# One index conversion for each row scatter instead of one for two, and a wider spread of the scatters over the batch

## The chip, the core and the metric

The kernel runs on one core of a Trainium2 chip. The metric is device time in microseconds (us). The core has five engines that work side by side, each through its own list of instructions in the order in which the program was built: TensorE (PE, with its weight loads PEld), VectorE (DVE), ScalarE (ACT), GpSimd (POOL) and SyncE (SP). Transfers run on 16 DMA engines and are issued from the lists of SP, ACT and POOL.

## What is computed

x has 8 batches of 512 rows of 256 numbers, in fp32. Four layers are added to it one after the other, each on layer-normed x:

```
x = x + scan(norm(x))         # silu(x Win), h = 0.9 h + x Bp, y = h Cp + D x, y Wout
x = x + ffn(norm(x))          # mixture of 16 experts, 4 chosen for each row, plus 2 shared
x = x + attention(norm(x))    # causal, 16 heads of 16
x = x + ffn(norm(x))          # the same mixture again
```

In the mixture each row picks 4 of 16 experts by its router scores. Its output is the weighted sum of what the four experts give, plus what the shared experts give.

## The kernel before

There are four stages. `stretch(Scan())` runs the scan layer over the 8 batches, and beside it, one and two batches behind, all of the first mixture that needs no sorted rows: the norm, the router scores, the choices and the shared experts. `routed(0, ...)` then runs the chosen experts of the first mixture on sorted blocks of 128 rows. `stretch(Attention())` and `routed(1, ...)` do the same for the attention and the second mixture.

Between a stretch and its `routed` lie the sorted rows. For each batch b the rows, normed, with their weights and numbers behind them, stand in a tile called `sorted_m` (buffer tag "rows", two buffers, so that batch b+2 takes the buffer of batch b). They are written to a table `xg` in device memory, 128 rows at a time, by an indirect DMA that POOL issues with 128 row positions (L656). A batch takes 16 of them: 4 tiles of rows by 4 choices. This text calls them the train of a batch, and m_0 to m_7 are the trains of the batches 0 to 7 of a stretch. The positions are computed in fp32 by DVE (`choices_w`, L633) and have to be unsigned integers. For the batches 0 to 6 ACT converts them (L653, `slots`), two columns for two scatters at a time, since PACE is 2; the conversion is kept at its place in ACT's list, so that a scatter can't start before ACT has come to that place. For batch 7 DVE converts all 16 columns at once (L635).

The place of each piece of work in the lists is set by `beside`, which merges generators by the share of their work that is done, and by `timed`, which gives each step a place between 0 and 1 of the batch of the layer (L1212 to L1250). The train of batch b-2 is dealt out in the loop over b: its last steps of choosing at 0.1, 0.14 and 0.18, and its 16 scatters from 0.22 on, spread towards 0.86 (towards 0.66 in the last batch; L1226). Then a scheduler puts the instructions in the lists by its own estimate of when they become ready; only the conversions are held where they were recorded.

Other work on POOL in the scan stretch is: adding the output bias to the next batch's x (L448, four instructions), writing the row numbers into the next `sorted_m` (an iota, L520, which has to wait until the last scatter out of that buffer has landed), and the power -1/2 of the norms (L400, `rstd_m` for the route and `rstd_l` for the layer). DVE waits for `rstd_m` before it writes `sorted_m` (L403), and its list goes on with the scan: L471, L473 (`state_s`) and L477. ACT scales by the skip weight (L474, after `state_s`), copies the transposed `sorted_m` out of PSUM (`xT_m`, L368), and PE then forms the router scores from it (`pl_m`, L543). In the attention stretch POOL also fills the values' tile with ones (L976, `v_a`).

SP stores each finished batch of x (L1193) and the shared experts' sums (L939).

Of the kernel before, what the change touches and what calls it, by code (L numbers as in the profile page):

```python
# [17 lines left out]
NT = T // P  # L18
# [11 lines left out]
EG, TKG, TK = 4, 2, 4  # L30
# [23 lines left out]
CLIP = 10.0  # L54
KB, COLS = 9, 6
HALVED = 1597463007.0
PACE = 2
SENT = 4
HELD = 6
EARLY = 2  # L60
# [12 lines left out]
def tile_hybrid_block(  # L73
# [22 lines left out]
    nc = tc.nc  # L96
# [38 lines left out]
    def rows_of(part, b: int):  # L135
        return part[b * T : (b + 1) * T, :].rearrange("(t p) d -> p t d", p=P)
# [168 lines left out]
    def behind(*pieces):  # L305
        def steps():
            for piece in pieces:
                yield from piece.steps

        return Piece(sum(piece.columns for piece in pieces), steps())  # L310
# [17 lines left out]
    def timed(steps, *places):  # L328


        def scaled():
            now = 0
            for place in places:
                yield place - now
                now = place
                next(steps)
            for _ in steps:
                pass

        return Piece(1, scaled())  # L340

    def spread(first: float, last: float, many: int):
        return [first + (last - first) * k / many for k in range(many)]

    def some(steps, many: int):

        for _ in range(many):
            yield next(steps)

    def issue(piece):  # L350
        for _ in piece.steps:
            pass


    def turned(src, tag: str, into, copies, home=None):

        rows = src()
        if home is None:
            dst = work.tile([P, KD, T], FP, tag="kb4", name=f"xT_{tag}", bufs=KB)
        else:  # L360
            dst = home(f"xT_{tag}")
        into(dst)
        for k in range(KD):
            pt = bank([P, NT, P], f"pt_{tag}_{k}")
            for t in range(NT):
                nc.tensor.transpose(pt[:, t, :], rows[:, t, k * P : (k + 1) * P], ident)
            flat = pt.rearrange("p t q -> p (t q)")
            copies[k](dst[:, k, :], flat)  # L368
            yield T // 2
# [38 lines left out]
    def kb4(name: str):  # L408
        return work.tile([P, NT, D], FP, tag="kb4", name=name, bufs=KB)
# [145 lines left out]
    def choices(i: int, b: int, tag: str, held, paced: bool):  # L555
# [65 lines left out]
        def of_choices(values, tag: str):  # L621
            found = work.tile(shape, FP, tag="col", name=f"found_{tag}", bufs=COLS)
            nc.vector.tensor_mul(
                found,
                pick,
                values.unsqueeze(2).to_broadcast(shape),
            )
            got = small.tile([P, NT, TK], FP, tag="choices", name=f"choices_{tag}")
            nc.vector.tensor_reduce(got, found, AX.X, ALU.add)
            return got  # L630

        slots = small.tile([P, NT * TK], U32, tag="slots", name=f"slots_{tag}")
        places = of_choices(where, f"w{tag}").rearrange("p t k -> p (t k)")  # L633
# [13 lines left out]
        for t in range(NT):  # L647
            for k in range(TK):
                at = t * TK + k
                if paced and at % PACE == 0:  # L650

                    pair = slice(at, at + PACE)
                    tc.keep_in_program_order(nc.scalar.copy(slots[:, pair], places[:, pair]))  # L653
                free(
                    f"xg{i}",
                    nc.gpsimd.indirect_dma_start(  # L656
                        out=xg[i],
                        out_offset=bass.IndirectOffsetOnAxis(ap=slots[:, at : at + 1], axis=0),
                        in_=rows[:, t, :],
                        in_offset=None,  # L660
                    ),
                )
                yield

    def free(group: str, made):

        tc.declare_no_dep(made.ins, group=group, reason="rows of their own")
        tc.add_to_no_dep_group(group, made.ins)
# [503 lines left out]
    def stretch(layer):  # L1172


        i = layer.mixture
        xT, xn, made, routes, sends = {}, {}, {}, {}, []

        def norm(b: int):
            def place():
                xn[b] = kb4(f"xn_{i}_{b}")  # L1180
                return xn[b]

            return normed(b, f"l{i}_{b}", place)

        def turn(b: int):
            return turned(lambda: xn.pop(b), f"l{i}_{b}", lambda xnT: xT.update({b: xnT}), layer.copies)

        def project(b: int):
            made[b], piece = layer.project(b, xT.pop(b))
            return piece  # L1190

        def store(b: int):
            nc.sync.dma_start(out=rows_of(parts[i][0], b), in_=x_tiles[b])  # L1193

        def experts(b: int):
            return shared_experts(i, b, lambda: routes.pop(b).held["xnT"], i == 1)

        for b in range(layer.ahead):
            if b < layer.early:
                xT[b] = ready.pop(b)  # L1200
            else:
                layer.load(b)
                issue(Piece(0, norm(b)))
                issue(Piece(0, turn(b)))
            if b == 0:
                issue(project(b))
        def start_route(b: int):
            routes[b] = Route(i, b, layer.copies)
            store(b)
            return routes[b]  # L1210

        for b in range(B):  # L1212
            pieces = [layer.main(b, made.pop(b))]
            nxt, last = b + layer.ahead, b == B - 1
            fill = []
            if layer.ahead > 1 and not last:
                fill.append(project(b + 1))
            if b > 1:
                shared_sum = experts(b - 2)
                if last:  # L1220

                    each = shared_sum.columns // 12
                    rest = Piece((12 - HELD) * each, shared_sum.steps)
                    shared_sum = Piece(HELD * each, some(shared_sum.steps, HELD))
                fill.append(shared_sum)
                pieces.append(timed(sends.pop(), 0.1, 0.14, 0.18, *spread(0.22, 0.66 if last else 0.86, NT * TK)))  # L1226
            if fill:
                pieces.append(behind(*fill))
            if b > 0:
                r = start_route(b - 1)  # L1230
                pieces.append(timed(r.norm(), *spread(0.0, 0.12, NT), *spread(0.2, 0.28, NT)))
                sends.append(r.rest)
                if last:
                    pieces += [
                        timed(r.scores(), 0.35, 0.38, *spread(0.45, 0.5, NT)),
                        timed(some(r.rest, PICKS), *spread(0.52, 0.66, PICKS)),
                        timed(some(r.rest, 3 + SENT), 0.69, 0.71, 0.73, *spread(0.75, 1.0, SENT)),
                    ]
                else:
                    pieces += [  # L1240
                        timed(r.scores(), 0.42, 0.46, *spread(0.55, 0.6, NT)),
                        timed(some(r.rest, PICKS), *spread(0.66, 0.95, PICKS)),
                    ]
            if nxt < B:
                layer.load(nxt)
                pieces += [
                    timed(norm(nxt), *spread(0.32, 0.44, NT), *spread(0.56, 0.64, NT)),
                    timed(turn(nxt), 0.75, 0.79),
                ]
            issue(beside(*pieces))  # L1250
            if layer.ahead == 1 and nxt < B:
                issue(project(nxt))
        layer.end()

        r = start_route(B - 1)
        chain = 3 + PICKS
        issue(
            beside(  # L1260
                behind(rest, experts(B - 2)),
                timed(r.norm(by_vector=True), *spread(0.0, 0.05, 2 * NT)),
                timed(sends.pop(), *spread(0.0, 0.5, NT * TK - SENT)),
                timed(r.scores(), 0.2, 0.22, *spread(0.28, 0.33, NT)),
                timed(some(r.rest, chain + 8), *spread(0.36, 0.68, chain), *spread(0.7, 1.0, 8)),
            )
        )
        table = []
        issue(
            beside(  # L1270
                experts(B - 1),
                timed(r.rest, *spread(0.0, 0.5, NT * TK - 8)),
                timed(blocks(i, table), 0.03, 0.14, 0.26, 0.38),
            )
        )
        return table

    with banks_of(one=8):
        table = stretch(Scan())
        wqkv_sb, wo_sb = load_attention_weights()  # L1280
# [90 lines left out]
```

## Time and profile before

| what | value |
|---|---|
| median of 3 runs | 1802.87 us (1798.23 to 1807.11) |
| profiled execution | 1817.59 us, span in the trace 1815.9 us |
| busy: PE, PEld | 93%, 70% of the span |
| busy: DVE, ACT, POOL | 60%, 44%, 42% |
| scan stretch | about 0 to 390 us |
| first routed stage | about 390 to 800 us |
| attention stretch | about 800 to 1383 us |
| second routed stage | about 1383 to 1816 us |
| scatters of rows (L656) | 256 on POOL, 255.4 us busy, 998 ns each |
| conversions by ACT (L653) | 112 of two columns, 19.4 us busy, 191 ns each |

A line of the profile's timeline has the start in us, the duration, the engine, the line of the code, the operation, what it writes and reads, how many instructions were merged into the line, and in square brackets the engine's idle time just before, with what ended it. A line of the table of stretches has the stretch, its length, then busy time and number of instructions of PE, PEld, DVE, ACT and POOL, and then the granted TensorE clock (1.00 is full), the busy share of the DMA engines and what they moved in GB/s.

### The profile page before, as it was taken

Reading aid. Unit: us, or ns where it says so; the run is one execution under the profiler, and the core shown is the slowest. Engines: PE = TensorE matmul, PEld = TensorE weight load, DVE = VectorE, ACT = ScalarE, POOL = GpSimd, SP = SyncE. Lnnn points to the kernel's source line nnn. Section 1 sums busy time; section 2 is a strip of 40 time slices with the busy share of each in tenths; the row PEclk is TensorE's granted clock in tenths of the full one; section 3 lists DMA queues with packets and bytes.
Section 4 is the critical chain, followed back from the end, with each engine's and each line's share of the span. In section 5 each row is a group of like instructions: output and inputs, shape, how many; then the busy total and the mean of one; then the engine's idle time right before and its main releaser. Section 6 shows DMA issues by size and latency. Waiting matters only on the chain. (4 is left out here: it accounts for less than half of the span.)

```text
span 1815.9 us, 32773 instructions
## 1 busy us (share of the span) xinstructions
PE 1694.6 (93%) x10640; PEld 1264.8 (70%) x10640; DVE 1088.1 (60%) x3364; ACT 805.3 (44%) x1740; POOL 763.0 (42%) x665
## 2 busy tenths in 40 slices
PE   5899998889999999989999999999988999999991
PEld 3566665569999999954445545544456999999991
DVE  5877775535555655556776676666643555555552
ACT  2322222125555555545564454454413555555550
POOL 4255554525555655540031321322551555565542
PEclk9899998989999999989999999999998999999995
DMA  5443322525566665540011112122542655566557
GB/s 162 151 149 131 130 78 85 178 77 95 96 97 102 108 97 94 94 88 12 24 58 63 61 64 69 50 72 72 178 147 62 97 97 94 107 118 97 97 105 240
DMA packets 149997, 181.37 MB, mean 100 GB/s; under 512 B 16096, under 2 KB 136960, under 8 KB 149824
## 3 DMA queue, kind: packets, MB, share of 16 engines
q0 software_dynamic: 53136, 76.81, 23.3%
q1 hardware_dynamic: 94320, 96.12, 17.8%
q10 hardware_dynamic: 2368, 6.29, 0.9%
q8 instruction: 89, 1.46, 0.3%
q14 instruction: 84, 0.69, 0.1%
HBM read 81.62 MB, written 97.53 MB: 99 GB/s over the span
## 5 line engine op out<-in xcount | busy, mean ns | idle before, releaser
L850 POOL DMA_INDIRECT part<-rows x272 | 426.4, 1568 | 388.2 <-ACT rows L849 339.9
L656 POOL DMA_INDIRECT xg<-sorted_m,slots_m x256 | 255.4, 998 | 298.2 <-ACT slots_m L653 120.2
L813 PEld LDWEIGHTS ph<-rows,gate 128*128 128x128 f32 x2176 | 286.3, 193 | 16.0 <-ACT rows L803 1.4
L813 PE MATMUL ph<-rows,gate 128*128 128x128 f32 x2176 | 289.7, 276 | 0.6 <-ACT rows L803 0.6
L813 PE MATMUL ph<-rows,up 128*128 128x128 f32 x2176 | 288.5, 276 | 0.0
L841 PE MATMUL pyr<-w_all,rows 128*128 x1088 | 281.9, 381 | 5.4 <-DVE rows L823 3.3
L813 PEld LDWEIGHTS ph<-rows,up 128*128 128x128 f32 x2176 | 266.0, 193 | 0.0
L821 ACT ACTIVATE rows<-ph 128x256 f32<-128x256 f32 x272 | 104.5, 384 | 333.1 <-PE ph L813 330.2
L822 DVE TENSOR_TENSOR rows<-ph,rows 128x256 f32<-128x256 f32 x272 | 115.5, 424 | 202.6 <-ACT rows L821 168.9
L841 PEld LDWEIGHTS pyr<-w_all,rows 128*128 128x128 f32 x1088 | 185.6, 191 | 20.6 <-issue 5.2
L795 ACT COPY gate<-w_all 128x512 f32 x272 | 170.0, 627 | 13.5 <-SPq L883 2.6
L1047 ACT ACTIVATE w_all<-ps_a 128x1024 f32<-128x1024 f32 x128 | 124.4, 1021 | 82.0 <-PE ps_a L1036 69.9
L902 PE MATMUL pg_m<-xT_m,su_sb 128*128 128x512 f32 x256 | 134.4, 650 | 5.2 <-ACT expert_b L736 5.2
L849 ACT ACTIVATE rows<-pyr,gain 128x256 f32<-128x256 f32 x272 | 128.7, 473 | 20.7 <-PE pyr L841 16.9
L795 DVE COPY up<-w_all 128x512 f32 x272 | 118.5, 436 | 32.1 <-PE ph L813 16.2
L1036 PE MATMUL ps_a<-w_all 32*128 32x512 f32 (+3 forms) x1024 | 123.3, 476 | 6.8 <-ACT w_all L1047 5.4
L930 PE MATMUL pd_m<-sd_sb,act_m 128*128 128x256 f32 x512 | 121.8, 386 | 4.5 <-DVE act_m L921 4.5
L902 PE MATMUL pg_m<-xT_m,sg_sb 128*128 128x512 f32 x256 | 123.0, 603 | 0.0
L823 DVE TENSOR_TENSOR rows<-ph,rows 128x256 f32<-128x256 f32 x272 | 115.2, 424 | 8.5
L826 DVE SCALAR_TENSOR_TENSOR gain<-rows,expert_b 128x4 f32<-128x4 f32 x272 | 60.4, 222 | 98.9 <-ACT rows L849 84.9
L802 PE MATMUL pt<-ident,rows 128*128 128x128 f32 x544 | 104.9, 275 | 12.8 <-DMA rows<-xg 12.8
L930 PEld LDWEIGHTS pd_m<-sd_sb,act_m 128*128 128x128 f32 x512 | 96.8, 192 | 27.2 <-DVE act_m L921 5.7
(208 smaller groups left out, 2205.3 us busy)
## 6 DMA issues: line engine op xcount, KB each, us to landing
rows<-xg SPq DMA_DIRECT2D x272, 136.0 KB
part<-x SPq DMA_DIRECT2D x16, 512.0 KB
part<-ys_m SPq DMA_DIRECT2D x16, 512.0 KB
w_all<-in_L_ffn_gate_w_dram SPq DMA_DIRECT2D x24, 256.0 KB
w_all<-in_L_ffn_up_w_dram SPq DMA_DIRECT2D x24, 256.0 KB
w_all<-in_L_ffn_down_w_dram SPq DMA_DIRECT2D x24, 256.0 KB
xg<-zeros SPq DMA_DIRECT2D x34, 136.0 KB
part<-rows POOLq DMA_INDIRECT x272
```

The source lines that it names most:

```text
L656: nc.gpsimd.indirect_dma_start(out=xg[i], out_offset=bass.IndirectOffsetOnAxis(ap=slots[:, at : at + 1], axis=0), in_=rows[:, t, :], in_of ...
L795: copy(here, w_all[:, bass.ds(held[n][0] + half * KD * F, KD * F)])
L813: nc.tensor.matmul(ph[:, s, f * P : (f + 1) * P], lhsT=both[s][:, k * F + f * P : k * F + (f + 1) * P], rhs=rows[:, ROW + k * P : ROW + (k ...
L822: nc.vector.tensor_mul(act, ph[:, 0, :], act)
L823: nc.vector.tensor_mul(act, ph[:, 1, :], act)
L841: nc.tensor.matmul(py, lhsT=act[:, f * P : (f + 1) * P], rhs=w_all[:, bass.ds(w + 2 * KD * F + f * D, D)], start=(f == 0), stop=(f == KF - 1),
L849: nc.scalar.mul(rows[:, 0:D], py, gain[:, TK : TK + 1])
L850: nc.gpsimd.indirect_dma_start(out=parts[i][n % 2], out_offset=bass.IndirectOffsetOnAxis(ap=rows[:, D + 2 * TK : D + 2 * TK + 1].bitcast(U ...
L902: nc.tensor.matmul(dst, lhsT=w[:, k, f * P : (f + 1) * P], rhs=xnT[:, k, :], start=(k == 0), stop=(k == KD - 1),)
L930: nc.tensor.matmul(py[:, j, :], lhsT=acts[n][:, f, t * P : (t + 1) * P], rhs=shared[n][3][:, f, :], start=(n == 0 and f == 0), stop=(n == ...
L1036: nc.tensor.matmul(ps[j // 2][:, j % 2, col : col + n], lhsT=k_sb[w][r, o, c * P : (c + 1) * P], rhs=q_sb[r, o, c * P : T], start=True, st ...
L1047: nc.scalar.activation(es[two], ps[two][:, :, 0:cols], AF.Exp, scale=ATT_SCALE)
```

## The change

PACE becomes 1: each of the 16 scatters of a paced batch has a conversion of its own, of one column, just ahead of it. The spread of the scatters goes from 0.22 to 0.86 (0.66 in the last batch) over to 0.26 to 0.98 (0.74 in the last batch), so that two neighbours stand 0.045 of a batch apart instead of 0.04. A variable gets another name.

```
-PACE = 2
+PACE = 1
...
                 if paced and at % PACE == 0:
-                    pair = slice(at, at + PACE)
-                    tc.keep_in_program_order(nc.scalar.copy(slots[:, pair], places[:, pair]))
+                    some_at = slice(at, at + PACE)
+                    tc.keep_in_program_order(nc.scalar.copy(slots[:, some_at], places[:, some_at]))
...
-                pieces.append(timed(sends.pop(), 0.1, 0.14, 0.18, *spread(0.22, 0.66 if last else 0.86, NT * TK)))
+                pieces.append(timed(sends.pop(), 0.1, 0.14, 0.18, *spread(0.26, 0.74 if last else 0.98, NT * TK)))
```

`spread(first, last, 16)` gives the places first + (last - first) k / 16 for k from 0 to 15.

## The prediction

> **What bounds the kernel now.** I read the table of stretches first: it shows where PE isn't full. Its columns are described above.
>
> ```profile
> 80.00:296.00 216.00, 204.64 (x755) 132.17 (x753) 162.27 (x474) 61.70 (x143) 105.12 (x115) 0.96 0.36 125
> ...
> 900.00:1296.00 396.00, 392.28 (x2439) 198.43 (x2432) 262.35 (x816) 198.37 (x321) 110.43 (x114) 0.99 0.19 64
> ```
>
> The first is the part of the scan stretch with trains, the second that of the attention stretch. In attention PE is idle for 3.7 of 396 us: there is nothing to win there, and something to lose only if ACT comes late. In the scan PE is idle for 11.4 of 216 us and runs below its full clock. So the scan decides, and I went through its timelines, POOL first. This is one batch, train m_1 and what follows it:
>
> ```profile
> 129.51 1.04 POOL L656 DMA_INDIRECT xg<-sorted_m,slots_m  x1 [13.20 <-DVE act_m L921]
> 130.85 1.16 POOL L656 DMA_INDIRECT xg<-sorted_m,slots_m  x1 [0.30 <-issue]
> 132.35 1.27 POOL L656 DMA_INDIRECT xg<-sorted_m,slots_m  x1 [0.33 <-ACT slots_m L653]
> ...
> 151.83 0.96 POOL L656 DMA_INDIRECT xg<-sorted_m,slots_m  x1 [0.30 <-DMA xg<-sorted_m,slots_m]
> 154.50 0.16 POOL L520 IOTA sorted_m<- 128x32 int32 x1 [1.71 <-DMA xg<-sorted_m,slots_m]
> 155.97 1.04 POOL L400 TENSOR_TENSOR rstd_m<-rstd_m,neg_half 128x4 f32<-128x4 f32 x1 [1.32 <-DVE rstd_l L399]
> ...
> 197.77 0.16 POOL L520 IOTA sorted_m<- 128x32 int32 x1 [2.91 <-DMA xg<-sorted_m,slots_m]
> 197.91 1.04 POOL L400 TENSOR_TENSOR rstd_m<-rstd_m,neg_half 128x4 f32<-128x4 f32 x1
> ```
>
> The train is not paced by ACT: after its third scatter it runs back to back, 0.96 us and a gap of 0.30, so 1.27 us a slot. POOL then waits for the landing, does the iota, and only then `rstd_m`. The next batch (197.77) shows the same. DVE stands still for it, and what follows on ACT and PE closes a ring:
>
> ```profile
> 198.99 1.38 DVE L403 TENSOR_SCALAR sorted_m<-x,mv_m,rstd_m 128x256 f32<-128x256 f32 x4 [5.35 <-POOL rstd_m L400]
> ...
> 131.27 0.72 ACT L474 ACTIVATE xi_s<-xi_s,d_sb 128x512 f32<-128x512 f32 x1 [2.27 <-DVE state_s L473]
> 131.90 0.27 ACT L653 CAST slots_m<-choices_wm 128x2 uint32<-128x2 f32 x2
> 132.07 0.57 ACT L368 COPY xT_m<-pt_m 128x512 f32<-128x512 f32 x1
> ...
> 132.70 0.39 PE L543 MATMUL pl_m<-rw_sb,xT_m 128*128 128x16 f32 x2 [0.97 <-ACT xT_m L368]
> 134.87 3.76 PE L902 MATMUL pg_m<-xT_m,su_sb 128*128 128x512 f32 x4
> ```
>
> From the end of `rstd_m` (115.18) DVE works without a pause to the fourth `state_s`; ACT's L474 waits for that, the copy `xT_m` stands behind it, and PE's `pl_m` waits for the copy. The first scatter starts 14.33 us after `rstd_m` ends (129.51 less 115.18), and the train leads to the next `rstd_m`. The ends of `rstd_m` lie at 115.18, 157.01, 198.95, 239.48 and 281.88: 41.7 us a batch. PE without pauses needs 38.5 (its first `pz_s` of two batches at 154.70 and 193.19). **The ring through POOL bounds the scan, not PE.** Every second batch PE is ahead and waits at `pl_m`; the table of stretches, cut just after that wait and at the same place a batch later, shows what comes of it:
>
> ```profile
> 134.00:139.00 5.00, 5.00 (x14) 2.93 (x13) 1.60 (x5) 0.00 (x0) 3.78 (x5) 0.50 0.30 113
> ...
> 174.00:179.00 5.00, 5.00 (x26) 3.44 (x25) 3.85 (x9) 2.10 (x9) 3.90 (x4) 1.00 0.30 111
> ```
>
> PE got half its clock after a pause of 0.97 and one of 0.18 us, and its batch took 42.2 us (`pl_m` from 132.70 to 174.91) instead of 38.5. (The Trainium skill, "TensorE: Matmul & The Clock Gate", section "What's actually happening", lets the clock fall only after about 3.4 us of idle. By the rule the longer pauses below would cost themselves alone, and a slow batch its pause in place of about 3.5 us more; the trace disagrees, and my sum goes by the ring.)
>
> **The change, part by part.**
>
> *Conversions.* 14 paced trains get 16 in place of 8: 112 more. One takes 191 ns, but neighbours start 0.09 us apart (two merged last 0.27), so each adds 0.1 of ACT's time, 11 us in all, spread over an engine that is 29% busy in the scan part above and 50% in the attention part. Nothing waits for most of them. In the scan one more stands between L474 and the first copy `xT_m`: 0.1 us at each wait of `pl_m`, but not on the ring.
>
> *The head of the train, scan.* By the built order the first conversion moves from behind the third L474 to just ahead of it (about 2 us earlier), and the next three stand behind the fourth L474, where two stood. The first scatter gains nothing: it waits for DVE (13.20, `act_m`), not for its conversion. The second one loses: it used the first pair, and now needs the conversion at 131.90. It can start where the third starts now, at 132.35 instead of 130.85. From there the train is back to back as before, so everything in it is **one slot later: 1.27 us** (bounds: nothing if the first scatter waited as long, and 132.35 to 133.92, 1.57, if the slow slot at the head recurs; I take 1.27, the rate of the other slots).
>
> *The tail of the train, scan.* The twelfth conversion follows the copy `xT_l` at 147.56, so at about 148.1; its scatter would be due at 146.76 + 1.27 = 148.03 and with the 0.45 us from conversion to scatter (131.90 to 132.35) starts at 148.5: 0.4 us more in the batches where PE was slow (m_1, m_3); in the others (conversion at 186.6, scatter due at 190.1) nothing. The last three stand behind `ys_m` (L938, 148.61 to 149.20) and are early enough. L448 moves from behind the tenth scatter to behind the eighth: the same 2.8 us in the train.
>
> *The sum in the scan.* Trains m_0 to m_4 are each followed by a `rstd_m`: 5 x 1.27 = 6.35. m_1 has 1.3 us to spare, since its `rstd_m` waited 1.32 for DVE: 5.05. Twice 0.4 for the tail: 5.85. 0.1 for the conversion ahead of the last `pl_m`: **6.0 us**. PE passes it on: at the last one it waits already (6.17 us at 295.93). Bounds: m_0, m_2 and m_4 alone, where `rstd_m` follows the iota at once, 3.8; all five at 1.57, no spare, plus the landing: the iota comes 2.67 us after the last scatter in m_1 and m_3, but 3.87 in m_0, m_2 and m_4, where SP's store of x falls in (issued at 192.45 for m_2). A later train may meet it each time: 2 x 1.2 more; 7.9 + 0.8 + 2.4 = 11.
>
> *Attention.* Trains run in groups of four with 5 us gaps that wait for ACT, so here the change does spread them. The last two conversions go behind `ys_m` (L938), which starts at 1038.18 where the last scatter now starts at 1032.03; iota about 1044. `rstd_m` is held by DVE anyway:
>
> ```profile
> 1048.61 1.08 POOL L400 TENSOR_TENSOR rstd_m<-rstd_m,neg_half 128x4 f32<-128x4 f32 x1 [12.60 <-DVE rstd_m L399]
> ```
>
> 4 us of cover are left; without it each later us would cost one. The fill of `v_a` moves ahead of the last two scatters; ACT needs it only at 1063.86. Of ACT's waits, 7.1 us for `choices_w` at the first conversion go, since that now stands behind two exponentials; PE didn't wait there. I take 0, between -3.7 (all of PE's idle time gone) and +5.6 (56 more conversions at 0.1, all uncovered).
>
> *Ends of both stretches.* Train m_6 ends 9 us (344.40 to 353.25) and 11 us (1329.10 to 1339.83) before m_7, which waits for its own DVE work: 0. The scatters of the trace have a median of 963 ns and a maximum of 1942, so I add nothing for a meeting with DVE. (A rule speaks against the wider spread: the Trainium skill, "SBUF — State Buffer", section "SBUF: two separate sides", says that a copy on DVE in its two-port mode keeps POOL from writing descriptors, so the more copies a train meets, the longer it takes. By it the sum would be higher; no row here shows a scatter held for longer than 1 us.)
>
> The profiled execution, 1817.6 us (span 1815.9 and 1.7 around it), would become 1823.6. It lies 14.7 above the median of the runs; I carry the 6.0 over to that: **1808.9 us**.
>
> **Rivals.**
>
> *A, the forecast:* one slot a batch in the ring, 1806.7 to 1813.9 by the bounds; 57%.
>
> *B, slower:* the train's end falls into the store of x in every batch, no spare is left, and PE pauses in each batch. Place: last scatter to iota in m_1 and m_3. Price: 11 us, 1813.9, with part of the conversions in attention uncovered up to 1819. It decides when the iota starts 3.8 us or more behind the last scatter in all five. For it: the store is issued at 154.68, 2.85 us after m_1's last scatter, and that moves towards it. Against: x, and so the store, comes later too when PE is late; 24%.
>
> *C, faster:* the ring opens and PE runs all five batches at 38.5 instead of 41.7: -16, 1786.9. It would need a train that ends earlier. The first conversion does come 2 us earlier, but DVE holds the first scatter; 7%.
>
> *D, no effect:* the train on POOL stays back to back, so the wider spread isn't followed, and the lost slot falls into waits of DVE and PE as it does in m_1: 0 to 2, 1803 to 1805; 12%.
>
> **Numbers.** Measuring tells about 0.5% (9 us) from no change. A and D are within it: 69%. B: slower, 24%. C: faster, 7%. The range runs from D less part of the runs' own scatter (4.6 us below their median, 4.2 above) to B's upper end plus as much: 1800 to 1822; C and the outermost of B are left out.
>
> **What would show it.** Right: in the scan a gap of about 1.5 us ahead of the second scatter of a train, then slots of 1.27; ends of `rstd_m` about 43 us apart, the fifth some 6 us later than 281.88, with the same start; in attention the sum of PE's idle time as before. Wrong: a second scatter that follows the first at 1.3 us; `rstd_m` still 41.7 apart; or pauses of PE in attention behind conversions.

## The result, and the profile after

| | before | after |
|---|---|---|
| median of 20 runs each | 1800.16 us (1797.06 to 1807.11) | 1805.07 us (1800.92 to 1810.60) |
| ratio, 95% interval | | 1.0021 [1.0012, 1.0031] |
| profiled execution, its span | 1817.59, 1815.9 us | 1800.94, 1799.2 us |

The change costs 3.8 us (2.2 to 5.6). The forecast had 6.0 us: the sign is right, the size lies outside the interval. The forecast held it likeliest that the time changes by less than 0.5%, which measuring couldn't tell from no change. 0.21% is less than that, but it is told from no change: the interval is clear of 1.

The two profiled spans point the other way, by 16.7 us, and have to be read with care. Before is longer by 9.3 us from the `pl_m` of the scan's batch 6 to the first matmul of the routed stage, and by 6.8 us from the last `pl_m` of the attention to the second routed stage. Neither belongs to the change: the kernel before took a median of 1802 us on one chip and 1822 to 1824 us on three others, and traces on these chips differ in just the same two sections (84 to 88 us against 96 to 101, and 55 against 60 to 64). So I compare sections, each from its own start, or traces of one chip.

The stage table after, the two rows shown of before:

```profile
80.00:296.00 216.00, 201.07 (x749) 130.27 (x747) 159.88 (x463) 62.18 (x177) 103.93 (x114) 0.97 0.35 124
...
900.00:1296.00 396.00, 391.11 (x2456) 196.06 (x2454) 264.15 (x830) 203.68 (x374) 111.59 (x115) 0.99 0.21 71
```

In the scan PE is idle for 14.9 us where it was 11.4; ACT has 34 instructions more there, and 53 in the attention. The table doesn't tell more: its stretches are cut at fixed times, and in the attention the two traces stand 9 us apart. POOL's timeline does; train m_1 and what follows it:

```profile
128.25 1.04 POOL L656 DMA_INDIRECT xg<-sorted_m,slots_m  x1 [13.20 <-DVE act_m L921]
131.09 1.27 POOL L656 DMA_INDIRECT xg<-sorted_m,slots_m  x1 [1.80 <-ACT slots_m L653]
132.66 0.96 POOL L656 DMA_INDIRECT xg<-sorted_m,slots_m  x1 [0.31 <-ACT slots_m L653]
...
148.00 0.96 POOL L656 DMA_INDIRECT xg<-sorted_m,slots_m  x1 [0.30 <-ACT slots_m L653]
149.26 0.96 POOL L656 DMA_INDIRECT xg<-sorted_m,slots_m  x1 [0.30 <-issue]
150.53 0.96 POOL L656 DMA_INDIRECT xg<-sorted_m,slots_m  x1 [0.30 <-issue]
151.79 0.96 POOL L656 DMA_INDIRECT xg<-sorted_m,slots_m  x1 [0.30 <-DMA xg<-sorted_m,slots_m]
155.60 0.16 POOL L520 IOTA sorted_m<- 128x32 int32 x1 [2.84 <-DMA xg<-sorted_m,slots_m]
155.74 1.04 POOL L400 TENSOR_TENSOR rstd_m<-rstd_m,neg_half 128x4 f32<-128x4 f32 x1
...
198.52 1.04 POOL L400 TENSOR_TENSOR rstd_m<-rstd_m,neg_half 128x4 f32<-128x4 f32 x1
```

The first scatter still waits 13.20 us for DVE. The second now waits 1.80 us, for a conversion; before it followed at 0.30. From there the train is back to back, and the first to the last scatter takes 23.54 us where it took 22.32. The ends of `rstd_m` lie 42.7 us apart on average, and the fifth 198.79 us behind the first scatter (before 193.94). PE and DVE pass it round, as they did before:

```profile
199.60 1.38 DVE L403 TENSOR_SCALAR sorted_m<-x,mv_m,rstd_m 128x256 f32<-128x256 f32 x4 [6.11 <-POOL rstd_m L400]
...
130.01 0.72 ACT L474 ACTIVATE xi_s<-xi_s,d_sb 128x512 f32<-128x512 f32 x1 [2.36 <-DVE state_s L473]
130.64 0.36 ACT L653 CAST slots_m<-choices_wm 128x1 uint32<-128x1 f32 x3
130.91 0.57 ACT L368 COPY xT_m<-pt_m 128x512 f32<-128x512 f32 x1
...
131.53 2.89 PE L543 MATMUL pl_m<-rw_sb,xT_m 128*128 128x16 f32 x12 [3.43 <-ACT xT_m L368]
```

PE waits 3.43 us at this `pl_m` (0.97 in before), and DVE 6.11 us for `rstd_m`. The attention, the row that answers to `rstd_m` at 1048.61 of before:

```profile
1030.05 0.96 POOL L656 DMA_INDIRECT xg<-sorted_m,slots_m  x1 [3.13 <-ACT slots_m L653]
1031.32 0.96 POOL L656 DMA_INDIRECT xg<-sorted_m,slots_m  x1 [0.30 <-issue]
1033.98 0.16 POOL L520 IOTA sorted_m<- 128x32 int32 x1 [1.70 <-issue]
1039.20 1.04 POOL L400 TENSOR_TENSOR rstd_m<-rstd_m,neg_half 128x4 f32<-128x4 f32 x1 [5.06 <-DVE rstd_m L399]
```

The cover of `rstd_m` shrank from 12.60 to 5.06 us and held. This whole stretch lies 9.1 us earlier than in before's trace, so the iota corresponds to 1043.1 there ("about 1044" was said).

### The profile page after: what moved, and what is told of

It reads as the page before. It is cut to its first block, busy times and chain, and to the rows that moved or that the text cites. A ratio compares the mean times of both kernels' runs of the same rounds, so it can differ in the third digit from the quotient of the medians.

```text
span 1799.2 us, 32953 instructions
## 1 busy us (share of the span) xinstructions
PE 1686.3 (94%) x10640; PEld 1261.1 (70%) x10640; DVE 1090.2 (61%) x3364; ACT 814.1 (45%) x1852; POOL 762.3 (42%) x665
## 3 DMA queue, kind: packets, MB, share of 16 engines
q10 hardware_dynamic: 2368, 6.29, 0.9%
## 5 line engine op out<-in xcount | busy, mean ns | idle before, releaser
L902 PE MATMUL pg_m<-xT_m,su_sb 128*128 128x512 f32 x256 | 130.8, 635 | 0.0
```

Of the source, the lines that this page charges most:

```text
L902: nc.tensor.matmul(dst, lhsT=w[:, k, f * P : (f + 1) * P], rhs=xnT[:, k, :], start=(k == 0), stop=(k == KD - 1),)
```

## Experiments

Theory: the slot that each train loses at its head goes round the ring through POOL and is the whole loss. Rivals: ACT's time for 112 more conversions; the later end of the train, with its landing; the attention. Each ratio is against the kernel before on the same chip.

### The two halves of the edit, and the two stretches

**a**: one conversion each, old places.

```
-spread(0.26, 0.74 if last else 0.98, NT * TK)
+spread(0.22, 0.66 if last else 0.86, NT * TK)
```

> One conversion for each scatter, at the old places (0.22 to 0.86, 0.66 in the last batch). In the built order the second conversion stands behind the third L474, where the first pair stood, so the second scatter has its index when DVE lets the first one go. Theory (the loss is the slot between the first and the second scatter of a train in the scan stretch): no such slot here, the second scatter follows the first at 0.3 us, L448 stays behind the tenth scatter, and the time is that of before within 1.5 us (ratio 0.999 to 1.001). Rival 'ACT's time' (112 conversions more cost ACT, and then PE, some 4 us): the whole loss is here, 1.002. Rival 'spread' (the loss comes from the later places, the end of the train above all): 1.000 as well, so this run doesn't tell it from the theory.

Measured: 0.9994 [0.9976, 1.0011].

**b**: pairs, new places (PACE = 2 in the changed kernel).

> Pairs as before, at the new places (0.26 to 0.98, 0.74 in the last batch). The first pair stands ahead of the third L474, the second behind the fourth, as the second pair did. Theory (the slot at the head): the first two scatters have their index early, the third waits as before, no slot is lost; 0.999 to 1.001. Rival 'spread' (the late end of the train meets the store of x, and L448 comes earlier): the whole loss is here, 1.002, with the iota of the row numbers 3.5 us or more behind the last scatter in every batch. Rival 'ACT's time': 1.000. If neither of the two halves alone shows the loss and the whole does, only the two together make the second scatter wait, as the theory has it.

Measured: 0.9972 [0.9952, 0.9993], faster than before.

**c**: the change in the scan stretch alone, and **d**: in the attention stretch alone.

```
+pace = PACE if i == 0 else 2        # d: i == 1
...
+*spread(0.26 if i == 0 else 0.22, (0.74 if last else 0.98) if i == 0 else (0.66 if last else 0.86), NT * TK)
```

> The whole change in the scan stretch, the old form in the attention stretch. Theory: the whole loss is here, about +4 us, ratio 1.001 to 1.003; a gap of 1.5 to 1.8 us ahead of the second scatter of each train, and the ends of rstd_m about 42.7 us apart. Rival 'attention' (56 conversions more and later scatters where PE has the least idle time): 1.000 here. Rival 'ACT's time': half the loss, +2 us.

Measured: 1.0042 [1.0022, 1.0062].

> The whole change in the attention stretch, the old form in the scan stretch. Theory: nothing, 0.999 to 1.001: rstd_m there is held by DVE, with some 4 us of cover behind the later end of the train, and PE's idle time stays at 4 to 5 us. Rival 'attention': the whole loss, 1.002. Rival 'ACT's time': half, +2 us.

Measured: 0.9995 [0.9972, 1.0017].

Neither half of the edit loses anything alone; only together do they put the second index behind the fourth L474. In a and b the second scatter starts 1.34 or 1.35 us behind the first in trains m_1 to m_4, in c 2.82 to 2.84. The loss is in the scan. Two things don't fit the theory: the scan alone costs more than the whole change, and b, which keeps the new places in the attention, beats before by some 5 us. Both point to the attention giving something back.

### Head of the train, and ACT's time

**e**: the change, but the first conversion covers two columns.

```
-if paced and at % PACE == 0:
+if paced and at != 1:
-    some_at = slice(at, at + PACE)
+    some_at = slice(at, 2 if at == 0 else at + 1)
```

> The change, but the first conversion of a train covers the first two columns, so the second scatter doesn't wait for a conversion behind the fourth L474; the other 14 have one each, at the new places. (One of the four L448 moves to behind the fifth scatter.) Theory (the slot at the head): the loss goes, 0.999 to 1.001 of before, the second scatter 0.3 us behind the first, the ends of rstd_m about 41.7 us apart. Rival 'spread' and rival 'ACT's time': 98 of the 112 conversions more and all later places are still there, so the loss stays, 1.002.

Measured: 1.0005 [0.9993, 1.0017]. Most or all of the loss goes, but not because the ring is as before: the fifth `rstd_m` ends 197.7 us behind the first scatter, not 194, and the `pl_m` of batch 6 starts 211.6 us behind it, 3.0 later than in before. The ends of `rstd_m` were to lie 41.7 us apart and lie 42.6 apart. So e's time alone doesn't show that the head is the whole loss; what the attention gives back (below) can hide what is left in the scan. POOL's timeline of e, train m_1, shows why:

```profile
130.89 1.04 POOL L656 DMA_INDIRECT xg<-sorted_m,slots_m  x1 [13.20 <-DVE act_m L921]
132.24 1.16 POOL L656 DMA_INDIRECT xg<-sorted_m,slots_m  x1 [0.30 <-issue]
133.73 1.26 POOL L656 DMA_INDIRECT xg<-sorted_m,slots_m  x1 [0.34 <-ACT slots_m L653]
...
149.88 0.96 POOL L656 DMA_INDIRECT xg<-sorted_m,slots_m  x1 [2.12 <-ACT slots_m L653]
...
154.94 0.96 POOL L656 DMA_INDIRECT xg<-sorted_m,slots_m  x1 [0.30 <-DMA xg<-sorted_m,slots_m]
158.72 0.16 POOL L520 IOTA sorted_m<- 128x32 int32 x1 [2.82 <-DMA xg<-sorted_m,slots_m]
```

The slot at the head is gone, and the train, now early, runs into the next conversion that is late: 2.12 us ahead of the twelfth scatter, 1.8 more than a slot's own gap. m_3 is as long (24.04 us from the first scatter to the last, m_1 24.05, the other trains 22.3 to 22.4). This is the wait that the forecast had at the tail; in the changed kernel the slot lost at the head had covered it.

**f**: before, with an idle second conversion behind each pair.

```
+spare_slots = small.tile([P, NT * TK], U32, tag="idle", ...)
...
 tc.keep_in_program_order(nc.scalar.copy(slots[:, pair], places[:, pair]))
+tc.keep_in_program_order(nc.scalar.copy(spare_slots[:, pair], places[:, pair]))
```

> The kernel before, with a second conversion of the same two columns into a tile that nobody reads behind each pair: 112 more on ACT, and no scatter waits for them. Theory: they cost nothing but 0.2 us at the copies xT_m, 0.999 to 1.001. Rival 'ACT's time': the whole loss, 1.002 or more.

Measured: 1.0019 [1.0008, 1.0030]: a miss for the theory. Two of the idle conversions stand between L474 and `xT_m` and delay the copy by 0.19 us (0.99 us from the start of L474 in f, 0.80 in before), and the `pl_m` of batch 6 is 0.9 us later from the first scatter than in before. That isn't the 3.4 us of the ratio. From there to the first routed stage f takes 88.4 us, and the other three traces of that chip (e, g, h) 84.0 to 86.3, but none of them is of the kernel before; where the rest arises stays open. It doesn't carry over to the change as such: a has 112 more conversions too, at no loss. But a conversion on ACT is free only where nothing behind it is waited for.

### The ring itself

**g**: before, with four buffers for `sorted_m`, and **h**: the same on the changed kernel.

```
-rows = work.tile([P, NT, ROW], FP, tag="rows", ...)
+if self.i == 0 and self.b % 2:
+    rows = values(...)[:, 0 : NT * ROW].rearrange("p (t c) -> p t c", t=NT)
+else:
+    rows = work.tile([P, NT, ROW], FP, tag="rows", ...)
```

> The kernel before, but in the scan stretch sorted_m of the odd batches lies in tiles that the attention uses later, so there are four buffers in place of two, and the iota of the row numbers no longer waits for the landing of the train just ahead of it on POOL. Theory (the ring through POOL bounds the scan, not PE): the 2.7 to 3.9 us between the last scatter and the iota go, a turn of the ring falls from 41.7 towards the 38.5 that PE needs, 39 to 40.5 a batch; 6 to 13 us faster, ratio 0.993 to 0.997. Rival 'PE bounds the scan' (its pauses at pl_m are then taken by something else): 1.000.

Measured: 0.9964 [0.9951, 0.9977].

> The changed kernel with the four buffers of the other run. Theory: still the slot at the head, so 0 to 6 us more than the four buffers without the change; below before in any case, ratio 0.994 to 0.999. With four buffers the end of a train no longer waits for its landing, so if the loss of the change lay in the landing (rival 'spread'), the two kernels with four buffers are equal.

Measured: 0.9996 [0.9982, 1.0010].

g's ratio falls where the theory had it, and h's just above, but not for its reason. The iota still waits 2.7 to 3.0 us behind the last scatter: with four buffers the scheduler moved it up by two batches, to behind the train that had last used its new buffer. From the first scatter to the `pl_m` of batch 6 g is only 2.6 us shorter. So g is no test of the ring; the next pair is.

**i** and **j**: as g and h, with the iota kept at its recorded place behind `rstd_m`.

```
-nc.gpsimd.iota(rows[:, :, D + 2 * TK :].bitcast(I32), ...)
+made = nc.gpsimd.iota(rows[:, :, D + 2 * TK :].bitcast(I32), ...)
+if self.i == 0:
+    tc.keep_in_program_order(made)
```

> The kernel before with the four buffers for sorted_m, and with the iota of the row numbers kept where it is recorded, behind rstd_m (with four buffers alone the scheduler had moved it one batch ahead, where it waited for the landing of the same train as before). Theory (the ring through POOL): the 1.7 to 3.3 us between the last scatter and the iota leave the ring now, a turn takes 14.3 + 22.3 + 1 + 1 = 38.6 to 39.5 us, about what PE needs, and the scan part is 8 to 13 us shorter than before's; with the iota of m_7 off the end of the stretch as well, ratio 0.991 to 0.995. Rival 'PE bounds the scan': no more than the four buffers alone gave (0.996).

Measured: 0.9905 [0.9887, 0.9922].

> The changed kernel with the four buffers and the iota kept behind rstd_m. Theory: a train is still one slot longer (1.27 us), a turn 39.9 to 40.8 us; POOL still bounds it, or PE nearly does: 3 to 6 us more than without the change. If a turn is then set by PE's 38.5 us, 0 to 2 us more. Below the kernel before, 0.993 to 0.998. Rival 'landing' (the loss of the change lies in the wait for the landing): no difference between the two.

Measured: 0.9949 [0.9929, 0.9969].

**k** and **l** are the kernel before and the changed kernel, on the same chip:

> The kernel before, unchanged, for a profile on the same chip as the others: 1.000. By the theory the ends of rstd_m lie at 27.2, 69, 111, 152 and 194 us behind the first scatter, within 1 us, and the second scatter follows the first at 1.34.

Measured: 0.9992 [0.9977, 1.0006].

> The changed kernel, unchanged, for a profile on the same chip as the others: 1.002. By the theory the ends of rstd_m lie at 28, 71, 113.6, 156 and 199 us behind the first scatter, within 1 us, some 5 us later at the fifth than in the kernel before; the rest of the program shows no difference of over 2 us in one direction.

Measured: 1.0020 [0.9995, 1.0045].

The end of train m_2 and what follows, on POOL, in i:

```profile
189.13 0.96 POOL L661 DMA_INDIRECT xg<-sorted_m,slots_m  x1 [0.30 <-DVE rstd_m L399]
190.11 1.05 POOL L400 TENSOR_TENSOR rstd_m<-rstd_m,neg_half 128x4 f32<-128x4 f32 x1
191.14 0.16 POOL L523 IOTA sorted_m<- 128x32 int32 x1
```

and in k, the kernel before:

```profile
191.85 0.96 POOL L656 DMA_INDIRECT xg<-sorted_m,slots_m  x1 [0.30 <-issue]
195.76 0.16 POOL L520 IOTA sorted_m<- 128x32 int32 x1 [2.95 <-DMA xg<-sorted_m,slots_m]
195.90 1.04 POOL L400 TENSOR_TENSOR rstd_m<-rstd_m,neg_half 128x4 f32<-128x4 f32 x1
```

With the wait for the landing out of the ring, `rstd_m` follows the train at once. The table of stretches from the first scatter to the `pl_m` of batch 6, k and then i:

```profile
85.66:294.48 208.82, 194.31 (x732) 126.69 (x730) 154.80 (x456) 57.37 (x136) 104.83 (x114) 0.97 0.34 117
```

```profile
87.85:283.06 195.21, 190.28 (x732) 124.31 (x731) 152.94 (x456) 58.08 (x136) 104.76 (x114) 0.99 0.36 126
```

The same 732 matmuls in 13.6 us less. PE's idle time falls from 14.5 to 4.9 us, and its clock rises from 0.97 to 0.99. The ends of `rstd_m` lie 38.9 to 39.4 us apart in i, 40.2 to 40.7 in j, 41.9 on average in k and 43.1 in l. The fifth is 6.5 us later in j than in i, and 6.1 us later in l than in k: five slots of 1.27, with almost nothing spared. **The ring through POOL bounds the scan, and the change lengthens it by one slot a turn**; shown by i against k and by j against i.

### What the attention gives back

**m**, **n**, **o**: scan alone, attention alone and both again, on one chip. **p**: i, with the change in the attention alone.

> The change in the scan stretch alone, a second time. Theory 'attention gives back': 5 to 7 us more than before (1.003 to 1.004), more than both parts together. Rival 'passed on in part': the same as both parts together, about 1.002.

Measured: 1.0045 [1.0027, 1.0063].

> The change in the attention stretch alone, a second time. Theory 'attention gives back': 1 to 4 us less than before (0.998 to 0.9995), four middle batches of 276.0 to 276.2 us between the pl_m. Rival 'passed on in part': 1.000.

Measured: 0.9982 [0.9954, 1.0009].

> The changed kernel again, beside its two halves on one chip: 1.002, and by both theories the sum of the two halves within 2 us.

Measured: 1.0019 [1.0002, 1.0035].

> Four buffers and the iota kept behind rstd_m, pairs at the old places in the scan, the change in the attention alone. Theory 'attention gives back': 1 to 4 us below the same kernel without the attention's part (0.9905 there), so 0.988 to 0.990, below both given kernels. Rival 'passed on in part': 0.9905.

Measured: 0.9884 [0.9856, 0.9912], the fastest kernel here: some 21 us below before.

Scan alone costs 1.0042 and 1.0045, both together 1.0021, 1.0020 and 1.0019: the attention takes off about 0.2%, some 4 us. Attention alone was below 1 both times, each time with an interval that holds 1. The traces are clearer. From the first `pl_m` of the attention to the sixth, ten traces with the new places there take 335.1 to 335.4 us, eight with the old ones 335.8 to 337.6. From there to the eighth they take 96.7 and 99.7 us on average.

The first difference, 1.1 us, can be seen. k, the first conversion of train m_2 (ACT, then PE):

```profile
1067.25 0.19 ACT L653 CAST slots_m<-choices_wm 128x2 uint32<-128x2 f32 x1 [1.78 <-DVE choices_wm L629]
1067.35 0.36 ACT L1006 COPY v_a<-pv_a 128x256 f32<-128x256 f32 x1
...
1067.76 1.13 PE L999 MATMUL pv_a<-w_att,xT_l 128*128 128x256 f32 x4 [0.33 <-ACT v_a L1006]
```

and the same place in l:

```profile
1076.52 0.37 ACT L1006 COPY v_a<-pv_a 128x256 f32<-128x256 f32 x1 [1.43 <-PE pv_a L999]
...
1076.99 1.13 PE L999 MATMUL pv_a<-w_att,xT_l 128*128 128x256 f32 x4
```

At the old place the conversion is early: ACT waits 1.78 us for DVE's `choices_w`, the copy `v_a` stands behind it, and PE waits for that copy. At the new place the conversion stands behind the copies and nobody waits. k has two such pauses (0.21 and 0.33 us). All eight traces with the old places have the first (0.21 to 0.30) and three of them the second; none of the ten with the new places has either. PE is idle for 2.1 us of this stretch on average with the old places and for 1.6 with the new ones: that is about half of the 1.1, and the rest is not accounted for.

The second difference goes by PE's clock. In every trace PE pauses for 1.01 us some 35 us behind the sixth `pl_m`. The 4 us after it, in k and in l:

```profile
1261.80:1265.80 4.00, 3.99 (x20) 1.87 (x20) 3.93 (x16) 2.94 (x5) 0.00 (x0) 0.76 0.18 62
1265.80:1269.80 4.00, 4.00 (x26) 1.14 (x24) 3.90 (x11) 1.70 (x4) 0.00 (x0) 0.50 0.02 6
```

```profile
1270.40:1274.40 4.00, 3.97 (x24) 1.80 (x28) 3.93 (x16) 3.37 (x5) 0.00 (x0) 1.00 0.22 62
1274.40:1278.40 4.00, 4.00 (x28) 1.50 (x20) 3.90 (x11) 2.92 (x4) 0.00 (x0) 1.00 0.01 3
```

The same pause costs half the clock in one and nothing in the other, and from the sixth `pl_m` to the seventh k takes 57.0 us, l 54.6. The clock fell right after it in 6 of 8 traces with the old places and in 2 of 10 with the new ones. That the change brings this about is likely by the counts (if places and clock had nothing to do with each other, so uneven a split would come about in 3 of 100 cases) and not shown: both outcomes occur with the old places and with the new ones.

## Why the prediction was right and wrong

- **What bounds the kernel**: right. i against k shows it by taking the landing out of the ring.
- **The head of the train**: right to the row. The gap ahead of the second scatter was to be about 1.5 us; it is 1.6 to 1.8. The first to the last scatter was to take 1.27 us more; it takes 1.2 to 1.5 more in each train.
- **The tail** (twice 0.4): did not occur. The scatters find their index 0.30 us after the one before. It is a real wait, 2.12 us in e, but PE reached it earlier from the first scatter than in before, and the lost slot covered it.
- **The spare of 1.3 us**: right in size, and used up: `rstd_m` of m_1's turn waited 1.32 us for DVE before and 0 after.
- **The landing** ("2 x 1.2 more" as an upper bound): about right as bounds go. From the last scatter's end to the iota m_1 and m_3 gained 1.14 and 0.96 us, and m_0, m_2 and m_4 lost 0.71, 0.34 and 0.67: +0.4 in all. Rival B needed five late landings; three of five became earlier. Its condition came about all the same: the store of x is now issued ahead of the end of the last scatter in all five trains, by 0.6 to 3.6 us (before in m_0, m_2 and m_4 alone). But the iota then waits 2.2 to 2.8 us, which is no more than the 2.9 of those three before.
- **The ring's sum**: five slots 6.29, landings +0.38, spare -1.32, and 0.5 less between m_3's `rstd_m` and the first scatter of m_4, which waited in before: 4.85 us. Over five traces with the change and four without, the `pl_m` of batch 6 is 5.6 us later from the first scatter (214.3 against 208.6). 6.0 was close.
- **The step that failed**: "Attention ... PE didn't wait there. I take 0". PE did wait, twice, for the copy that stood behind the early conversion; both waits are in before's trace as well (0.21 and 0.34 us, at 925.87 and 1064.28), and I looked at ACT's waits without asking what stood behind them. In place of 0 the attention gives back some 4 us, just beyond the bound of -3.7 that I had for it: 7.9 us with the change in the scan alone, 3.8 with both. The traces put 1.1 of it between the first and the sixth `pl_m`, half of that pauses of PE that are gone, and 3.0 in the two batches behind, where the clock differs; that the clock's part is the change's doing isn't shown. This is the second wait in before's trace:

```profile
1063.76 0.19 ACT L653 CAST slots_m<-choices_wm 128x2 uint32<-128x2 f32 x1 [1.79 <-DVE choices_wm L629]
1063.86 0.37 ACT L1006 COPY v_a<-pv_a 128x256 f32<-128x256 f32 x1
...
1064.28 1.13 PE L999 MATMUL pv_a<-w_att,xT_l 128*128 128x256 f32 x4 [0.34 <-ACT v_a L1006]
```

To name what is queued behind a waiting instruction is needed for a wait that is removed as well as for one that is added.

- **"Measuring tells about 0.5% (9 us) from no change"**: too coarse. 20 runs of each kernel gave an interval of 0.19%, so even 0.21% is clear of no change.
- What remains: the scan alone costs some 7.9 us (1.0042 and 1.0045 of 1822), of which the ring explains 5.6. From the `pl_m` of batch 6 to the routed stage traces of one chip show 0 to 2 us more with the change, in single executions; that remainder stays open. So 3.8 lies near 6.0 in part by luck: some 2 us that the sum didn't have, and 4 that it didn't take off.

## What to carry to other kernels

A train of work that runs back to back on one engine isn't spread by new places in the list; what the places move is the instruction that each piece waits for. Follow each index to its first user, on both sides: a conversion too late costs its queue, one too early costs whatever stands behind it. Where an engine's list closes a ring, take out the wait in it that nothing needs: the iota moved behind `rstd_m`, with four buffers, gave 17 us, over four times what the change cost.

## What the hardware showed that I had not expected

- The clock after a pause isn't decided by the length of the pause alone. After 1.01 us at the same place it fell to 0.50 or stayed at 1.00. In the scan of the changed kernel the pauses of 1.02, 1.10 and 1.08 us were followed by 1.00, and those of 3.43, 3.76 and 6.75 us by 0.50 to 0.54; in the kernel before a pause of 0.97 was followed by 0.50. (The Trainium skill, "TensorE: Matmul & The Clock Gate", section "What's actually happening", says that activity is judged in free-running windows of about 3.4 us, so that the moment counts. The same pause with two outcomes agrees with that; a fall after about 1 us of idle doesn't agree with its one idle window.)
- One program, two levels of chips: 1802 and 1822 us, the difference in the sections where the stretches end and the routed stages begin. Profiles from two chips can't be subtracted as a whole.
- The landing of an indirect scatter of 128 rows isn't constant: the iota came 1.7 to 3.3 us after the end of the last scatter in the scan, in one and the same kernel.
